# Two sequences' tokens at once: seven half products for the candidate's and the input gate's x part instead of eight

## The chip, the cores and the metric

The kernel runs on one core of a Trainium2 chip as one launch. The metric is device time in microseconds of one execution. The kernel before takes 2463.74 us, the median of three runs (2462.84 to 2463.92).

The engines are named as the profile names them: PE is TensorE's matmuls, PEld its weight loads, DVE VectorE, ACT ScalarE, POOL GpSimd, SP SyncE (which here mostly issues DMAs). Each engine works through its own instructions in order.

## The reference

The program is two layers on 32 sequences of 128 tokens of 512 values: layer 0 is a mixture of experts and a feed-forward part, layer 1 an expert stage that gives `r * y`, and then a recurrence. The change lies in the recurrence alone:

```python
x = x + L0_ffn(L0_cond(x, cond, ...), ...)
x = x + L1_ffn(L1_cond(x, token_ids, cond, ...), ...)

def L1_ffn(x, wf, uf, bf, wi, ui, bi, wc, uc, bc, wo, uo, bo, in_c):
    def step(c, xt):                       # x: (32, 128, 512); scan over the 32
        ft = sigmoid(xt @ wf.T + c @ uf.T + bf)
        it = sigmoid(xt @ wi.T + c @ ui.T + bi)
        gt = tanh(xt @ wc.T + c @ uc.T + bc)
        return ft * c + it * gt, None      # c: (128, 512)
    c_final, _ = lax.scan(step, broadcast(in_c), x)
    return tanh(x @ wo.T + c_final @ uo.T + bo)
```

One step takes one sequence: its 128 tokens are the batch, and the state c (128 x 512) goes from sequence to sequence. The x part of a gate, `xt @ w.T`, needs no c and can be computed ahead; the c part can't.

## The kernel before

All layers are one program. The change touches its last part, from the block `with sf:` (L1515) to the end of the body; the order of instructions ahead of it stays, but for one DVE instruction.

**Products in three parts.** A factor is split in a high part (ACT copies it to a shorter type, L64) and a low part (DVE subtracts that from the source, L65); `split` does both. `mm3` (L76 to L86, the matmul at L82) then multiplies high by high, high by low and low by high: three matmuls per block of 128 of the summed dimension. A product of 128 tokens x 512 by 512 x 512 is four blocks, so twelve matmuls with 128x512 results; a half product, over two blocks, is six.

**A step t of the recurrence** (loop at L1663). Three gates c, i, f, one PSUM bank each. `from_c` (L1591) adds the c part, `gate` (L1596) adds the bias on DVE (L1598), applies tanh or sigmoid on ACT (L1599) and multiplies i by c (L1601); `new_c` (L1602) makes the new c in two DVE instructions (L1604, L1606). PE must then wait for the new c, and gets other work in the meantime: the x part of c and i of step t + 1 (`from_x`, L1583, 24 matmuls), then the transposes of the new c (`turn`, ptC, L1578, followed by its split to cT), then the x part of f (12 matmuls) and the transposes of a later sequence (`gate_y`, ptF, L1566). So a step is 36 matmuls of the c part, 36 of the x part and eight transposes. The order is written out in the loop.

**Where z comes from.** z is `r * y` transposed and split. `get_y` (L1538 to L1546) gathers the rows of y on POOL's queue and loads r on SP's queue; `gate_y` (L1556) applies the sigmoid to r, multiplies (L1561), transposes, copies to zt (L1571), stores that to DRAM for the output stage (L1572) and splits it. `gate_y` runs two steps ahead (LEAD = 2). The last two of the eight groups of four sequences stay on the chip.

**Weights.** `weight` (L1494 to L1508) loads a matrix in two halves of 512 KB into a pool of raw tiles (`zop`, four slots) and splits each: casts of 128x1024 on ACT, subtracts on DVE. Before the stage, wc, uf and wi are loaded while the expert stage still runs, wf on POOL's queue during the first products; the expert stage's last outputs are copied by ACT to ob (L1465) and stored to `res_d`, from which y is gathered. wo is loaded after step 4.

**Banks of PSUM.** `ps_g` four (gates and output units), `ps_c` one (ptC), `ps_y` one (ptF), `ps_z` two (not used).

**The last steps and the output.** From step 29 on there is no x part left to do: the x part of step 31 is done at t = 29 and put by (L1688), and PE fills its waits for c with output units (`unit`, L1611: twelve matmuls with wo) of group 6, whose results ACT copies to SBUF. Then `cu` (L1724), the c part of the output from the last c and uo, then the other 28 units, group by group; groups 0 to 5 are loaded back (`fetch_z`, L1624) and split. `result` adds cu on DVE (L1729), applies tanh on ACT (L1732), adds x1 (L1733, by turns on DVE and POOL) and stores (L1734).

## Time and profile before

| | |
|---|---|
| median of three runs | 2463.74 us |
| the profiled execution's own time | 2462.88 us |
| its span in the profile | 2461.1 us |
| mean granted clock of TensorE | 0.995 |
| PE busy | 2421.7 us, 12870 matmuls |
| DVE busy | 1349.3 us, 2309 instructions |
| ACT busy | 1051.4 us, 1852 instructions |
| POOL busy | 408.9 us, 462 instructions |

The span runs from the first to the last instruction in the profile; 1.8 us of the execution lie around it. The recurrence takes the time from about 1795 to 2364 us of the span, the output from there to the end. Where the chain of waits is shown, a row is a start in us from the span's beginning, a length in us, an engine, the tile written, the line, and how many instructions. In the timeline, the square bracket behind a row tells how long the engine had been idle and which instruction released it. A clock of 1.00 is TensorE at its full clock.

### The profile page before, as it was taken

How to read it: one execution, taken by the hardware profiler on the slowest of the kernel's cores; microseconds unless marked ns; L12 is line 12 of the kernel's file. 1: busy time of each engine (PE TensorE's matmuls, PEld its weight loads, DVE VectorE, ACT ScalarE, POOL GpSimd, SP SyncE). 2: the span in 40 equal slices, each digit the busy share in tenths (PEclk: the TensorE clock that was granted, in tenths of full speed). 3: DMA queues.
4: the chain of work that ended last, by engine and by line, in shares of the span. 5: the costliest groups of instructions: out<-in, count | busy, mean ns of one | idle time of the engine just before them, and what ended most of it. 6: DMA issues, size and time to landing. Idle time of an engine off the chain costs nothing.

```text
span 2461.1 us, 36619 instructions
## 1 busy us (share of the span) xinstructions
PE 2421.7 (98%) x12870; PEld 2048.8 (83%) x12870; DVE 1349.3 (55%) x2309; ACT 1051.4 (43%) x1852; POOL 408.9 (17%) x462
## 2 busy tenths in 40 slices
PE   8999999999999999999999999999999999999998
PEld 6788788888888788888888889999978888888887
DVE  8896654556557454455454567667643333333363
ACT  5544533344224544455455466666532222222142
POOL 1000022221232233322223010000010000000012
PEclk9999999999999999999999999999999999999999
DMA  6445555557565343342342487777532111110164
GB/s 214 152 125 177 183 167 169 178 176 233 176 215 170 95 131 111 125 152 68 117 142 95 152 285 223 230 231 224 172 132 69 42 49 48 43 43 30 32 212 158
DMA packets 194125, 353.73 MB, mean 144 GB/s; under 512 B 37457, under 2 KB 70273, under 8 KB 191377
## 3 DMA queue, kind: packets, MB, share of 16 engines
q1 hardware_dynamic: 145392, 253.33, 31.4%
q0 software_dynamic: 36448, 75.95, 10.4%
q10 hardware_dynamic: 12096, 22.03, 2.5%
q8 instruction: 108, 1.77, 0.3%
q14 instruction: 81, 0.66, 0.1%
HBM read 374.99 MB, written 89.70 MB: 189 GB/s over the span
## 4 chain that ended last, share of the span: by engine, by line
PE 49%; issue 2%; DMA 1%; POOL 1%; DVE 1%; ACT 1%; POOLq 0%; DVEq 0%; ACTq 0%
PE phD L82 7%; PE ps_c L82 7%; PE ps_f L82 7%; PE ps_i L82 7%; PE poD L82 7%; PE po L82 3%; PE pb L82 2%; PE pv L82 2%; POOL hF L1733 1%; PE ptC L1578 1%; PE ptD L1431 1%; PE ptF L1566 1%; PE poF L82 0%; PE ptB L1256 0%; DMA rowsD<-xk_d,slot_t 0%
## 5 line engine op out<-in xcount | busy, mean ns | idle before, releaser
L65 DVE TENSOR_TENSOR wD<-rawD,wD 128x1024 fp32r<-128x1024 f32 x128 | 156.6, 1230 | 82.5 <-ACT wD L64 82.5
L82 PE MATMUL p<-xhl,swu 128*128 128x512 f32 x768 | 189.0, 397 | 5.9 <-ACT xhl L64 5.8
L82 PEld LDWEIGHTS phD<-xe,wD 128*128 128x128 f32 x1536 | 184.4, 189 | 2.1 <-ACT xe L64 0.9
L82 PE MATMUL phD<-xe,wD 128*128 128x256 f32 x1536 | 185.1, 281 | 0.7 <-ACT xe L64 0.7
L82 PE MATMUL p<-xhl,kept_u 128*128 128x512 f32 x768 | 184.3, 394 | 0.7 <-DVE kept_u L65 0.7
L82 PE MATMUL poD<-wD,hD 128*128 128x512 f32 x768 | 181.5, 392 | 0.0
L82 PEld LDWEIGHTS p<-xhl,swu 128*128 128x128 f32 x768 | 144.7, 190 | 36.1 <-ACT xhl L64 5.8
L82 PEld LDWEIGHTS p<-xhl,kept_u 128*128 128x128 f32 x768 | 141.9, 188 | 30.0 <-DVE kept_u L65 1.1
L82 PEld LDWEIGHTS poD<-wD,hD 128*128 128x128 f32 x768 | 141.9, 188 | 28.3
L64 ACT CAST wD<-rawD 128x1024 fp32r<-128x1024 f32 x128 | 133.3, 1046 | 56.0 <-PE poD L82 54.0
L290 POOL DMA_INDIRECT xg<-in_x_rows_dram,blk_t x71 | 67.6, 952 | 443.2 <-PE ptx L300 246.3
L1538 POOL DMA_INDIRECT y<-res_d,gat_i x32 | 30.4, 951 | 511.8 <-DVE r L1561 432.3
L82 PE MATMUL pur<-r,xb 128*128 x792 | 110.5, 288 | 4.2 <-ACT xb L64 1.1
L82 PE MATMUL por<-r,hbr 128*128 x396 | 107.9, 407 | 1.1 <-ACT hbr L64 1.1
L65 DVE TENSOR_TENSOR xb<-ptx,xb 128x512 fp32r<-128x512 f32 x68 | 47.0, 691 | 106.0 <-ACT xb L64 104.3
L82 PEld LDWEIGHTS pur<-r,xb 128*128 128x128 f32 x792 | 98.5, 189 | 6.4 <-issue 2.1
L82 PE MATMUL ps_f<-wf_hl,z 128*128 128x512 f32 x384 | 96.2, 399 | 0.0
L82 PE MATMUL ps_c<-uc_hl,cT 128*128 128x512 f32 x384 | 96.2, 399 | 0.0
L82 PE MATMUL ps_c<-wc_hl,z 128*128 128x512 f32 x384 | 94.8, 396 | 1.4 <-ACT z L64 1.4
L82 PE MATMUL pb<-rT,Wo_hl 128*128 128x256 f32 x768 | 95.2, 281 | 0.3 <-DVE rT L65 0.2
L82 PE MATMUL acc<-swd,as 128*128 128x512 f32 x384 | 94.7, 391 | 0.7 <-DVE as L65 0.6
L815 POOL DMA_INDIRECT o<-o_d,s_i x64 | 66.7, 1042 | 172.3 <-PE pth L835 84.4
(1020 smaller groups left out, 4991.3 us busy)
## 6 DMA issues: line engine op xcount, KB each, us to landing
rawD<-in_w_key_dram SPq DMA_DIRECT2D x64, 512.0 KB, 4.3
rawD<-in_w_value_dram SPq DMA_DIRECT2D x64, 512.0 KB, 4.3
swr<-in_sw_dram SPq DMA_DIRECT2D x120, 256.0 KB, 3.5
o_d<-obr SPq DMA_DIRECT2D x66, 256.0 KB, 2.4
rraw<-in_rw_dram SPq DMA_DIRECT2D x32, 256.0 KB, 3.1
xc<-in_x_dram SPq DMA_DIRECT2D x32, 256.0 KB, 3.6
hid_d<-o ACTq DMA_DIRECT2D x32, 256.0 KB, 2.2
xh_d<-xc SPq DMA_DIRECT2D x32, 256.0 KB, 2.8
```

What stands on the lines that cost most here:

```text
L64: first = nc.scalar.copy(hi, src).ins
L65: done = nc.vector.tensor_tensor(lo, src, hi.bitcast(F32), ALU.subtract).ins
L82: done = nc.tensor.matmul(ps, lhsT=left(hl, k), rhs=right(hr, k), start=start and k + n == 0, stop=stop and 3 * k + n == last,)
L290: nc.gpsimd.indirect_dma_start(out=xg[i], out_offset=None, in_=a["x_rows"], in_offset=bass.IndirectOffsetOnAxis(ap=blk_t[:, i : i + 1], ax ...
L815: nc.gpsimd.indirect_dma_start(out=o[n], out_offset=None, in_=o_d, in_offset=bass.IndirectOffsetOnAxis(ap=idx[:, b : b + 1], axis=0),)
L1431: nc.tensor.transpose(pt[:, k, :], xe[:, s, bass.ts(k, P)], ident)
L1538: got = nc.gpsimd.indirect_dma_start(out=y, out_offset=None, in_=res_d, in_offset=bass.IndirectOffsetOnAxis(ap=gat_i[:, b : b + 1], axis=0),)
L1566: nc.tensor.transpose(pt[:, k, :], r[:, bass.ts(k, P)], ident)
L1578: nc.tensor.transpose(pt[:, k, :], c[:, bass.ts(k, P)], ident)
L1733: (nc.gpsimd if n % 2 else nc.vector).tensor_tensor(h, h, x1s[g][:, :, o, :], ALU.add)
```

## The change

For two sequences 2n and 2n + 1, let A1, A2 be the halves of the first sequence's z along the summed dimension, B1, B2 the second's. Let c0, c1 and i0, i1 be the halves of wc and wi. Needed are four products of two halves each:

- first, c: A1 c0 + A2 c1; first, i: A1 i0 + A2 i1;
- second, c: B1 c0 + B2 c1; second, i: B1 i0 + B2 i1.

That is eight half products of six matmuls. After the change they are seven, as in the product of two 2x2 matrices with seven multiplications (Winograd's form): A1·c0, A2·c1, S1·T1, S2·T2, S3·T3, S4·i1, A2'·T4, where the S are sums of halves of z, made by DVE per pair, and the T are sums of halves of wc and wi, made once. (In the code the rows of the left matrix are the two sequences: A11, A12 the first's halves, "A22" the second half of the second's; B11 = c0, B21 = c1, B22 = i1.) The products are put together by eight more DVE additions per pair. The gate f keeps its plain product.

- **Pair 0** is computed plainly, c from B11 and B21 (12 matmuls), and i from B11, T1 = i0 - c0 and B22 (18 matmuls), since i0 itself is no longer kept. Pairs 1 to 15 take the seven products.
- **In the loop**, after an odd step five of the seven products (`first_of_pair`, 30 matmuls) stand ahead of the transposes of c and f's 12 behind; after an even step S3·T3 and f (6 + 12) stand ahead and A22·T4 (6) behind.
- **Two additions** of `second_i` are held behind the new c by an explicit order (`issue_after(made[0])`).
- **Weights**: nine half tiles in place of three whole pairs. B11, B21, T1, B22 and f0, f1 are made at the start; for T2, T3, T4 the halves of wi and wc are loaded again after step 0 (`rest_of_weights`). At t = 1 the bias of i becomes bi - bc.
- **z**: `gate_y` copies all of z to zt and stores all groups to DRAM; two are done after step 0, then one per step, three ahead. The first zt takes the buffer of the first cT.
- **Banks**: `ps_g` three, `ps_b` three (for the half products), `ps_c` and `ps_y` one each.
- **The end**: x parts go on to step 31, so no unit is left as filler there; wo is loaded at t = 28, uo after the loop; all eight groups are loaded back and computed in order, their units by turns in `ps_g` and `ps_b`; two units stand ahead of cu; the last result's addition of x1 is on DVE instead of POOL.

The diff, cut to its core:

```diff
+        def sums_z(n):
+            zt = zts[n]
+            a1, a2 = zt[:, 0, :K2], zt[:, 0, K2:]
+            b1, b2 = zt[:, 1, :K2], zt[:, 1, K2:]
+            s = gp.tile([P, 2, K2, P], F32, tag="sz", name=f"sz_{n}")
+            nc.vector.tensor_tensor(s[:, 0], b1, b2, ALU.add)
+            nc.vector.tensor_tensor(s[:, 1], s[:, 0], a1, ALU.subtract)
+            split(zS[n][:, 0:2, 0], zS[n][:, 0:2, 1], s)
+            nc.vector.tensor_tensor(s[:, 1], a2, s[:, 1], ALU.subtract)
+            nc.vector.tensor_tensor(s[:, 0], a1, b1, ALU.subtract)
+            split(zS[n][:, 2:4, 0], zS[n][:, 2:4, 1], s)
...
+        def first_of_pair(n):
+            first, second, c1 = (zop.tile([P, 2, D], F32, tag="raw", name=f"{x}_{n}") for x in ("ta", "tb", "pa"))
+            p1, u, v = first[:, 0], first[:, 1], second[:, 0]
+            nc.vector.tensor_tensor(p1, block("A11", "B11", n), bias["c"], ALU.add)
+            nc.vector.tensor_tensor(c1[:, 0], block("A12", "B21", n), p1, ALU.add)
+            nc.vector.tensor_tensor(v, block("S1", "T1", n), bias["i"], ALU.add)
+            nc.vector.tensor_tensor(u, block("S2", "T2", n), p1, ALU.add)
+            nc.vector.tensor_tensor(v, v, u, ALU.add)
+            nc.vector.tensor_tensor(c1[:, 1], block("S4", "B22", n), v, ALU.add)
+            parts[2 * n] = {"c": c1[:, 0], "i": c1[:, 1]}
+            half_done[n] = u, v
+
+        def second_i(n):
+            c2 = zop.tile([P, 2, D], F32, tag="raw", name=f"pd_{n}")
+            u, v = half_done[n]
+            p7 = block("S3", "T3", n)
+            with tc.issue_after(made[0]):
+                nc.vector.tensor_tensor(u, p7, u, ALU.add)
+                nc.vector.tensor_tensor(c2[:, 1], p7, v, ALU.add)
+            parts[2 * n + 1] = {"c": c2[:, 0], "i": c2[:, 1]}
+
+        def second_c(n):
+            u, _ = half_done.pop(n)
+            nc.vector.tensor_tensor(parts[2 * n + 1]["c"], block("A22", "T4", n), u, ALU.add)
...
+        c0, i0 = raw_part("wc", 0), raw_part("wi", 0)
+        split_part("B11", c0)
+        c1 = raw_part("wc", 1)
+        split_part("B21", c1)
+        nc.vector.tensor_tensor(i0, i0, c0, ALU.subtract)
+        split_part("T1", i0)
+        i1 = raw_part("wi", 1)
+        split_part("B22", i1)
         uc["f"] = weight("uf", uf_p, zop, 4)
-        wx["i"] = weight("wi", wx_p, zop, 4, pair=wx_hl["i"])
...
+        def rest_of_weights():
+            with tc.issue_after(last_r[0]):
+                i0, i1, c0, c1 = (raw_part(n, h) for n in ("wi", "wc") for h in range(2))
+            nc.vector.tensor_tensor(i0, i1, i0, ALU.subtract)
+            nc.vector.tensor_tensor(c0, i0, c0, ALU.add)
+            split_part("T2", c0)
+            nc.vector.tensor_tensor(c1, c1, c0, ALU.subtract)
+            split_part("T3", i0)
+            split_part("T4", c1)
...
-            if t < NB - 2:
-                from_x(t + 1, ps, "ci", True, False)
-            cT_next = turn(c, t + 1)
-            if t < NB - 2:
-                from_x(t + 1, ps, "f", True, False)
-            for b in ((t + LEAD,) if t < NB - 4 else (NB - 2, NB - 1) if t == NB - 4 else ()):
+            n, odd = divmod(t + 1, 2)
+            if t == 0:
+                for w in "ci":
+                    plain(1, ps, w, True, False)
+                cT_next = turn(c, t + 1)
+                plain(1, ps, "f", True, False)
+            elif t < NB - 1:
+                if odd:
+                    second_i(n)
+                    plain(t + 1, ps, "f", True, False)
+                else:
+                    first_of_pair(n)
+                cT_next = turn(c, t + 1)
+                if odd:
+                    second_c(n)
+                else:
+                    plain(t + 1, ps, "f", True, False)
+            else:
+                cT_next = turn(c, t + 1)
+            for b in (2, 3) if t == 0 else (t + 3,) if t + 3 < NB else ():
                 gate_y(b)
                 if b + LEAD < NB:
                     get_y(b + LEAD)
+                if b % 2:
+                    sums_z(b // 2)
+            if t == 0:
+                rest_of_weights()
```

`block` is six matmuls of one half product into a bank of `ps_b`, `plain` the six-matmul halves added into a gate's bank, `raw_part` one load of 512 KB into a slot of `zop`, and `split_part` its split.

## The prediction

> **What bounds the kernel now.** I read the page's busy shares first. TensorE (PE) works 98% of the span, so time moves by what PE no longer does or by holes that open in it.

> ```profile
> PE 2421.7 (98%) x12870; PEld 2048.8 (83%) x12870; DVE 1349.3 (55%) x2309; ACT 1051.4 (43%) x1852; POOL 408.9 (17%) x462
> ```

> Then busy time by stretch of the last stage (columns: stretch, us, busy us and instructions of PE, PEld, DVE, ACT, POOL; granted clock; DMA share; GB/s). The recurrence is one stretch without a hole; its start and the turn to the output products run at a lower mean clock:

> ```profile
> 1828.00:2346.00 518.00, 518.00 (x2396) 428.27 (x2395) 187.61 (x273) 125.83 (x204) 24.56 (x26) 1.00 0.16 50
> 1795.00:1813.00 18.00, 14.93 (x59) 11.63 (x58) 6.87 (x8) 9.13 (x14) 7.28 (x10) 0.84 0.66 225
> 2367.00:2388.00 21.00, 20.44 (x101) 18.01 (x100) 14.68 (x23) 11.04 (x23) 3.84 (x3) 0.84 0.77 257
> ```

> Third, the chain of waits inside the recurrence (start, us, what). It never leaves PE: twelve matmuls take 2.72 us, so one takes 2.72 / 12 = 0.2267, and four transposes 0.44.

> ```profile
> 2318.77 2.72 PE ps_f L82 x12
> 2321.49 2.72 PE ps_c L82 x12
> 2324.21 2.72 PE ps_i L82 x12
> ...
> 2335.09 0.44 PE ptC L1578 x4
> ```

> A step of 72 matmuls and two sets of transposes takes 72 x 0.2267 + 0.88 + about 0.05 = 17.25 us, while DVE is busy 187.6 / 518 x 17.25 = 6.2 us and ACT 4.2.

> Last, the timeline of one step, for what stands between the last product and the next transposes:

> ```profile
> 1836.84 0.69 DVE L1598 TENSOR_TENSOR v_f<-ps_f,bf_bc 128x512 f32<-128x512 f32 x1 [0.64 <-PE ps_f L82]
> 1837.56 0.63 ACT L1599 ACTIVATE v_f<-v_f 128x512 f32<-128x512 f32 x1 [2.09 <-DVE v_f L1598]
> 1838.23 0.69 DVE L1604 TENSOR_TENSOR v_f<-v_f,c 128x512 f32<-128x512 f32 x1 [0.70 <-ACT v_f L1599]
> 1838.95 0.69 DVE L1606 TENSOR_TENSOR c<-v_f,v_i 128x512 f32<-128x512 f32 x1
> 1842.08 0.60 PE L1578 MATMUL ptC<-ident,c 128*128 128x128 f32 x4
> ```

> Call T the end of f's matmuls (1836.64, where the next PE row starts). The state c is ready at T + 3.00; ptC comes at T + 5.44: 24 matmuls cover the gate with 2.4 us to spare.

> **1. Matmuls: -17.7 us.** Eight half products (48 matmuls) per pair become seven (42) for 15 pairs: 90 fewer. Pair 0 stays plain with three halves for i instead of two, 6 more in each of two sequences: +12. 78 x 0.2267 = 17.7, at full clock and with PE never waiting. Groups of six instead of twelve should not cost more each: the expert stage changes its output tile every six matmuls and runs 36 in 8.42 us with the overlapped end of its last (8.42 - 0.23 = 8.19, or 0.2275 each).

> ```profile
> 1695.33 8.42 PE L82 MATMUL poD<-wD,hD 128*128 128x512 f32 x36
> ```

> **2. The steady steps: 0.** Added per pair on DVE: 8 adds of 128x512 (the row of L1598, 0.69; the gates keep their own adds, with another operand): 5.5 us; two splits of 128x512 (DVE 0.69 each, ACT 0.59) and four 128x256 adds at 0.42 (the layer-0 rows of that size). That is 5.5 + 1.4 + 1.7 = 8.6 us a pair, 4.3 a step: DVE goes to some 10.5 of a 16.6 us step, ACT to 5. Neither fills. What counts is order:
> - First kind of step (odd t; filler 30 matmuls, then ptC at T + 6.80). DVE does v_f's add, then A11's add (T + 1.56 to 2.25) ahead of v_f times c: c at T + 4.39, 2.4 us to spare. A11's bank is wanted back at T + 4.08 and A12's at T + 5.44; their adds end at 2.25 and about 3.7.
> - Second kind (even t; filler 6 + 12, ptC at T + 4.08). The two adds on p7 are held behind new c, so c stays at T + 3.00: 1.1 us to spare. The split of c's transpose ends at T + 6.0 (0.59 and 0.69 after ptC); from_c starts at T + 6.3 and uses its low half at T + 6.8.
> The cover is thus 1.1 us in every other step; if it is gone, each microsecond beyond it costs 15.

> **3. Start of the stage: +4.4 (+2 to +7).** In the order of the built program ACT copies the expert outputs ob ahead of the weight casts (it was the other way round), and uf's two raw halves need slots of a pool of four that the c and i halves hold.

> ```profile
> 1795.69 0.58 ACT L1465 COPY ob<-poD 128x512 f32<-128x512 f32 x1
> ...
> 1803.76 0.69 DVE L1561 TENSOR_TENSOR r<-y,r 128x512 f32<-128x512 f32 x1 [6.72 <-DMA y<-res_d,gat_i]
> ...
> 1808.38 1.22 PE L82 MATMUL ps_c<-wc_hl,z 128*128 128x512 f32 x2 [1.37 <-ACT z L64]
> ...
> 1810.25 4.22 PE L82 MATMUL ps_c<-wc_hl,z 128*128 128x512 f32 x10
> ```

> Before, all casts of uf, wc and wi were done when ob was copied. Now five casts of 1.05 us (B11, B21, T1, B22 and uf's first half) follow it; one of them stands ahead of the second store of ob, which moves the gather of y by 1.05. uf's loads leave at about 1799.7 and 1801.3 and land 4.7 to 7.0 later (rows of wc and uf); behind them on ACT stand the two casts of wf, whose loads on POOL's queue are now behind two bias loads and land at about 1809; their casts end at 1810.95. Then come r_2's sigmoid 0.63, zt 0.59, z's cast 0.62: the first x products start near 1812.95 instead of 1808.38, and the ten of c at 1814.7 instead of 1810.25: +4.4. Low end: loads as quick as wc's and wf's fastest. High end: the uf loads as slow as 7.0 with the casts behind them, which adds 2.5.

> **4. The rest of the weights: +4.3 (0 to +7).** T2, T3, T4 are made from wi and wc read again, issued on SP's queue behind r_5's load, which waits for ptF_3 (about 1838.5). Four loads of 512 KB that landed in 3.3 to 4.7 us at the same rate before are there at 1843 to 1847. DVE takes its queue in order: a subtract and an add of 128x1024 and three low halves at 1.22 stand ahead of v_f times c of step 1 or 2. I make c ready at 1854.4 where PE could transpose at 1851.9: 2.5, and 0.3 for a bank of the same chain; both nearest to the cast rows. A gap also lowered the clock at the start (half clock for the 4.22 us of ten matmuls that take 2.27): I add 1.5 for a part of such a stretch. Low end: the loads 3 us earlier, no gap. High end: 4 us and a whole stretch (2.0 to 3.4).

> **5. The turn to the output, and the end: +1.3 - 0.6 (-4 to +5).** Before, from the end of the last f (2360.64) to 2452.5 the matmuls' own time falls 4.2 us short, by one gap and the low clock after it:

> ```profile
> 2366.78 2.79 PE L82 MATMUL cu<-cT,uo_hl 128*128 128x128 f32 x24
> 2370.14 5.16 PE L82 MATMUL cu<-cT,uo_hl 128*128 128x128 f32 x24 [0.56 <-ACT cu L1724]
> ```

> Now uo's casts and the casts of zF_1 and zF_2 stand in ACT's and DVE's queues ahead of step 31's sigmoid and products. I make c ready at T + 5.6 with ptC reached at T + 4.3 (1.35 wait), 0.45 for c's low half, 0.85 at cu_3 and the same low clock after it (2.8): 5.5 instead of 4.2. If the clock stays up there, it is 4 less. The last sum moves from POOL (1.26 us at L1733) to DVE (0.69): -0.6.

> **Weighed against the trace.** The clock fell to 0.50 at 2372 to 2376 although PE's gap before was 0.56 us. [...]

> **Sum.** -17.7 + 4.4 + 4.3 + 1.3 - 0.6 = -8.3. The profiled execution took 2462.88 us (span 2461.1, 1.8 around it), so 2454.6; the median of the three runs is 2463.74, 0.9 above, so 2455.4. I say 2455.0.

> **Rivals.**
> - The edges are hidden: terms 3 to 5 at their low ends, +2, 0 and -4 to 0, leave -17.7 + 2 - 2.5 to 0: 2445 to 2448. For it: loads here land anywhere from 3.3 to 7.0 us. Against: ACT's order at the start is fixed.
> - The edges take most of it: high ends +7, +7, +4 make -17.7 + 18 = 0; half-way to them, 2459 to 2464, within 0.2%. For it: three places where in-order queues meet fresh loads.
> - Slower: the steady steps stall. Place: ptC of the second kind of step, or the third bank of S2 and S4. Price: 15 us for each microsecond of DVE delay beyond the 1.1 spare; from 0.9 beyond it (2.0 in all) the sum passes +4.9. If short gaps of each pair cost a half-clock stretch as at 2370 (5.16 us for 24 matmuls against 2.79, so 2.4 to 3.4), it is 15 x 3 - 8 = +37: 2500. Against: the adds on p7 are held back behind new c, and the gaps are none if the order above holds. [...]
> - The products save nothing, because six matmuls and a change of tile cost what eight do: 2475. The poD row excludes nearly all of it.

> **Chances.** Forecast (2449 to 2459) 0.53; edges hidden 0.18; edges take most 0.19; steady stall 0.08; nothing saved 0.02. A measurement of this kernel can tell about 0.2%, 4.9 us: faster below 2458.8, slower above 2468.7. So faster 0.71, same 0.19, slower 0.10. The range takes in the hidden and the dear edges: 2446 to 2464; the stall lies outside.

> **What would show it.** 78 fewer PE instructions, all steps between 1830 and 2350 without PE idle at clock 1.00 and 16.6 us mean; DVE at about 10.5 us a step; ps_c's ten matmuls of t = 0 4 us later; one wait of ptC for c near 1852; one at step 31. Wrong if ptC waits for DVE in every even step, if the granted clock between 1860 and 2340 is below 1.00, or if p and S tiles show idle before them released by DVE.

## The result and the profile after

The changed kernel takes 2453.65 us (median of 6 runs, 2447.08 to 2457.65) against 2464.26 for the kernel before (6 runs, 2462.84 to 2468.64): the medians are 10.6 us apart, and the ratio of the runs is 0.995, with a 95% interval of 0.9934 to 0.9966. The forecast was 2455.0, faster.

The profiled execution of the changed kernel took 2457.65 us, its slowest run, so its span (2456.0) is only 5.1 us shorter. The order of instructions ahead of the last stage is the same in both kernels, and yet the stage's first product (`ps_c<-uc_hl`) starts at 1801.10 instead of 1795.70: 5.4 us. I don't count them to the change. The low-clock stretches ahead of it (where the granted clock is 0.5) add up to 13.7 us instead of 6.8, worth 3.4 us by an estimate (half of the 6.8 more, at a granted clock of 0.5), and in the other profiles of the changed kernel and its versions the stage starts anywhere from 1794.2 to 1804.0 us. With only two profiles of the kernel before (1795.7 and 1795.9) this is likely and not shown. So all that follows is measured from that first product to the end of the span: 654.9 us after, 665.4 before, 10.5 less.

First the page's line of busy shares: 78 matmuls fewer, and 239 DVE instructions more, 140 us.

```profile
PE 2407.7 (98%) x12792; PEld 2036.4 (83%) x12792; DVE 1488.9 (61%) x2548; ACT 1079.0 (44%) x1897; POOL 412.0 (17%) x461
```

Then busy time by stretch (columns as before): the steady steps, the start, and steps 1 and 2, where T2, T3 and T4 are made.

```profile
1890.00:2340.00 450.00, 450.00 (x2086) 372.24 (x2085) 280.80 (x444) 131.43 (x215) 24.54 (x22) 1.00 0.15 47
1801.10:1832.00 30.90, 23.07 (x87) 17.35 (x86) 15.49 (x17) 15.82 (x20) 10.71 (x11) 0.89 0.63 213
1832.00:1883.40 51.40, 47.10 (x209) 38.51 (x209) 34.34 (x53) 18.43 (x29) 4.04 (x4) 0.93 0.31 103
```

In the steady steps PE has no hole and the clock is 1.00, with DVE busy 62% of the time. Both edges have holes. The waits of PE between 1790 us and the end name them (us in total, times, longest):

```profile
PE ptF L1572 <- ACT zt L1574: 6.8, 2, 3.5
PE ps_f L82 <- ACT uf_hl L64: 2.8, 2, 2.4
PE ps_f L82 <- DVE uf_hl L65: 1.8, 2, 1.0
PE ptC L1594 <- DVE c L1675: 1.4, 2, 0.8
PE cu L82 <- ACT cu L1849: 0.5, 1, 0.5
```

The timeline shows where they stand. At the start ACT casts the halves of wc behind the copies of ob; uf's first load leaves at 1804.12, f's c part waits for it, wf's casts follow, and zt_0's copy comes behind all of them:

```profile
1801.78 1.05 ACT L64 CAST wB_hl<-raw_wc 128x1024 fp32r<-128x1024 f32 x1
...
1804.12 0.33 SPq L1504 DMA_DIRECT2D raw_uf<-in_uf_dram  x1
...
1809.13 0.49 PE L82 MATMUL ps_f<-uf_hl,cT 128*128 128x512 f32 x1 [2.43 <-ACT uf_hl L64]
...
1820.19 0.66 PE L1572 MATMUL ptF<-ident,r 128*128 128x128 f32 x4 [3.26 <-ACT zt L1574]
```

In step 1 the weights read again land late, and zt_4's copy stands behind three casts of them on ACT; PE stands at the transposes that need its bank:

```profile
1855.21 1.23 DVE L1722 TENSOR_TENSOR raw_wi<-raw_wi,raw_wi 128x1024 f32<-128x1024 f32 x1 [3.12 <-DMA raw_wi<-in_wi_dram]
...
1861.43 0.58 ACT L1574 COPY zt<-ptF 128x512 f32<-128x512 f32 x1
...
1862.06 1.11 PE L1572 MATMUL ptF<-ident,r 128*128 128x128 f32 x4 [3.50 <-ACT zt L1574]
...
1863.97 1.11 PE L1594 MATMUL ptC<-ident,c 128*128 128x128 f32 x4 [0.80 <-DVE c L1675]
```

At the end there are two short waits and, unlike before, no low clock behind them (the stretch 2355 to 2370 has 1.00).

For the comparison of runs the stage is cut by its transposes of c. ptC_n is the start of the transposes of c_n; every run has the same four pieces (us, from the PE rows of each profile):

| run | first product to ptC_1 | ptC_1 to ptC_5 | ptC_5 to ptC_30 | ptC_30 to the end | stage |
|---|---|---|---|---|---|
| before | 29.1 | 69.2 | 441.0 | 126.2 | 665.4 |
| changed | 37.8 | 75.5 | 415.8 | 125.8 | 654.9 |
| e1 plain pairs | 37.5 | 69.7 | 432.3 | 130.4 | 669.9 |
| e2 weights early | 38.5 | 68.2 | 415.8 | 125.9 | 648.5 |
| e3 T3, T4 later | 39.4 | 72.9 | 415.8 | 125.9 | 653.9 |
| e4 uf first | 32.8 | 73.6 | 415.8 | 125.9 | 648.1 |
| e5 both | 32.5 | 68.2 | 415.8 | 126.3 | 642.9 |
| e6 changed again | 38.8 | 73.6 | 415.8 | 126.0 | 654.1 |
| e7 one more on DVE | 38.7 | 73.8 | 415.8 | 130.4 | 658.7 |
| e8 three more on DVE | 38.6 | 74.9 | 420.0 | 126.2 | 659.7 |
| e9 before again | 29.3 | 69.2 | 442.5 | 126.8 | 667.9 |
| e10 last add on POOL | 38.5 | 73.1 | 415.8 | 128.8 | 656.2 |
| e11 both, cu mixed | 32.5 | 68.3 | 415.8 | 125.4 | 642.0 |
| e12 six more on DVE | 38.5 | 77.9 | 420.5 | 131.4 | 668.1 |

The kernel before does step 31's x part (36 matmuls, 8.2 us) in the third piece, the changed kernel (24 matmuls, 5.4 us) in the fourth. All output units lie in the fourth piece in both.

### The profile page after: what moved, and what is told of

It reads as the page before. It is cut to its first block, busy times and chain, and to the rows that moved or that the text cites. A ratio compares the mean times of both kernels' runs of the same rounds, so it can differ in the third digit from the quotient of the medians.

```text
span 2456.0 us, 36828 instructions
## 1 busy us (share of the span) xinstructions
PE 2407.7 (98%) x12792; PEld 2036.4 (83%) x12792; DVE 1488.9 (61%) x2548; ACT 1079.0 (44%) x1897; POOL 412.0 (17%) x461
## 3 DMA queue, kind: packets, MB, share of 16 engines
q0 software_dynamic: 36448, 75.95, 10.4%
## 4 chain that ended last, share of the span: by engine, by line
PE 53%; DMA 2%; DVE 1%; ACT 1%; issue 0%; SPq 0%; POOL 0%; DVEq 0%; ACTq 0%
PE phD L82 7%; PE poD L82 7%; PE ps_f L82 7%; PE po L82 4%; PE ps_c L82 4%; PE ps_i L82 4%; PE poF L82 3%; PE pS L82 3%; PE pb L82 2%; PE pA L82 2%; PE pv L82 2%; PE ptC L1594 1%; PE ptD L1431 1%; PE ptF L1572 1%; PE ptB L1256 0%; PE pr L1176 0%
## 5 line engine op out<-in xcount | busy, mean ns | idle before, releaser
L82 PE MATMUL p<-xhl,swu 128*128 128x512 f32 x768 | 189.1, 397 | 5.7 <-ACT xhl L64 5.7
L82 PEld LDWEIGHTS phD<-xe,wD 128*128 128x128 f32 x1536 | 185.5, 190 | 2.1 <-ACT xe L64 0.9
L82 PE MATMUL phD<-xe,wD 128*128 128x256 f32 x1536 | 186.2, 282 | 0.7 <-ACT xe L64 0.7
L82 PE MATMUL p<-xhl,kept_u 128*128 128x512 f32 x768 | 184.2, 394 | 0.7 <-DVE kept_u L65 0.7
L82 PE MATMUL poD<-wD,hD 128*128 128x512 f32 x768 | 181.6, 392 | 0.0
L82 PEld LDWEIGHTS p<-xhl,swu 128*128 128x128 f32 x768 | 144.7, 190 | 36.1 <-ACT xhl L64 5.7
L82 PEld LDWEIGHTS p<-xhl,kept_u 128*128 128x128 f32 x768 | 141.9, 188 | 30.0 <-DVE kept_u L65 1.1
L82 PEld LDWEIGHTS poD<-wD,hD 128*128 128x128 f32 x768 | 141.9, 188 | 28.3
L64 ACT CAST wD<-rawD 128x1024 fp32r<-128x1024 f32 x128 | 133.4, 1047 | 56.8 <-PE poD L82 35.0
L1540 POOL DMA_INDIRECT y<-res_d,gat_i x32 | 36.5, 1140 | 489.4 <-DVE r L1564 410.9
L82 PE MATMUL pur<-r,xb 128*128 x792 | 111.8, 290 | 4.4 <-issue 1.5
L82 PE MATMUL por<-r,hbr 128*128 x396 | 108.2, 408 | 1.3 <-ACT hbr L64 1.2
L82 PEld LDWEIGHTS pur<-r,xb 128*128 128x128 f32 x792 | 99.6, 190 | 6.9 <-issue 2.9
L82 PE MATMUL ps_f<-uf_hl,cT 128*128 128x512 f32 x384 | 94.2, 393 | 4.6 <-ACT uf_hl L64 2.8
L82 PE MATMUL ps_c<-uc_hl,cT 128*128 128x512 f32 x384 | 96.2, 398 | 0.0
L82 PE MATMUL pb<-rT,Wo_hl 128*128 128x256 f32 x768 | 95.2, 281 | 0.3 <-DVE rT L65 0.2
L82 PE MATMUL acc<-kept_d,as 128*128 128x512 f32 x384 | 93.5, 391 | 1.2 <-ACT as L64 0.7
L82 PE MATMUL pv<-w_recept_hl,xr 128*128 128x512 f32 x384 | 94.4, 395 | 0.0
```

The costliest lines, as they stand in the source:

```text
L64: first = nc.scalar.copy(hi, src).ins
L82: done = nc.tensor.matmul(ps, lhsT=left(hl, k), rhs=right(hr, k), start=start and k + n == 0, stop=stop and 3 * k + n == last,)
L1540: got = nc.gpsimd.indirect_dma_start(out=y, out_offset=None, in_=res_d, in_offset=bass.IndirectOffsetOnAxis(ap=gat_i[:, b : b + 1], axis=0),)
```

## The experiments

**e1: all pairs plain.** What do the seven products bring by themselves?

```diff
-                "i": ((0, "B11"), (0, "T1"), (1, "B22")),
+                "i": ((0, "T1"), (1, "B22")),
-        nc.vector.tensor_tensor(i0, i0, c0, ALU.subtract)
...
-            if t == 0:
+            if t < NB - 1:
                 for w in "ci":
-                    plain(1, ps, w, True, False)
+                    plain(t + 1, ps, w, True, False)
...
-                if b % 2:
-                    sums_z(b // 2)
-            if t == 0:
-                rest_of_weights()
```

> All pairs as plain products: c and i take 24 matmuls of x part per sequence again, no sums of z, no T2, T3, T4, the bias of i unchanged; banks, loads at the start, filler places and the end as in the changed kernel. Theory A (each matmul left out is worth 0.2267 us, steady steps have no stall, the weights read again cost about 7.2 us): 2453.65 + 17.7 - 7.2 = 2464.2, within 3 us of the kernel before; steady step 17.25 us; no PE wait near 1860. Theory B (the seven products save nothing, the gain came from the new end of the kernel): 2446 to 2454.

Measured: 2466.2 us against 2463.5 before, ratio 1.0011 (1.0000 to 1.0021). Theory A holds; two transposes of c in a row stand 17.29 us apart:

```profile
2005.14 0.60 PE L1594 MATMUL ptC<-ident,c 128*128 128x128 f32 x4
...
2022.43 0.60 PE L1594 MATMUL ptC<-ident,c 128*128 128x128 f32 x4
```

In the third piece the seven products save 432.3 - 415.8 = 16.5 us, where the 72 matmuls that it holds fewer (1728 instead of 1800) make 16.3 at 0.2267. The new start is still there without them (37.5), the wait in step 1 is not (69.7): the one comes with the half tiles and their loading, the other with T2 to T4. The start even holds 12 matmuls (2.7 us) fewer than in the changed kernel; in this profile the low clock there lasts 13.7 us, in the changed kernel's 6.8.

**e2: the weights read again, early.**

```diff
+        with tc.issue_after(last_r[0]):
+            raws = [raw_part(n, h) for n in ("wi", "wc") for h in range(2)]
         cT_next = cT
         for t in range(NB):
...
-            with tc.issue_after(last_r[0]):
-                i0, i1, c0, c1 = (raw_part(n, h) for n in ("wi", "wc") for h in range(2))
-            nc.vector.tensor_tensor(i0, i1, i0, ALU.subtract)
+            i0, i1, c0, c1 = raws
+            with tc.issue_after(made[0]):
+                nc.vector.tensor_tensor(i0, i1, i0, ALU.subtract)
```

> The four loads for T2, T3, T4 are issued ahead of the loop instead of after r_5's load, and their sums on DVE start behind c_1. Theory A (PE waits at 1858 to 1865 because the loads land at 1855 and their casts then stand ahead of zt_4 and of v_f times c): the waits of 3.5 and 0.8 us go and so does the low clock behind them, 6 to 7 us faster than the changed kernel, 2446.5 to 2448. Rival (the order of the queues alone makes the wait, loads or not): the wait moves to step 0 or 1, 2452 to 2455.

Measured: 2443.46 us, ratio 0.992 (0.9904 to 0.9935). The second piece is 68.2, 7.2 less than in the changed kernel's first profile and 5.4 less than in its second, and the low clock near 1862 is gone. For the wait, theory A holds. The median fell by 10.2, to 3.0 below the expected range, which is more than the stage shows (5.6 to 6.4 us shorter). Between the two profiled executions, 4.7 of 11.1 us lie ahead of the stage: it starts at 1796.4 us of the span in this profile and at 1801.1 and 1799.1 in the two of the changed kernel.

**e3: the same late loads, T3 and T4 behind c_2.**

```diff
             split_part("T2", c0)
-            nc.vector.tensor_tensor(c1, c1, c0, ALU.subtract)
-            split_part("T3", i0)
-            split_part("T4", c1)
+            return i0, c0, c1
...
+                with tc.issue_after(made[0]):
+                    nc.vector.tensor_tensor(c1, c1, c0, ALU.subtract)
+                    split_part("T3", i0)
+                    split_part("T4", c1)
```

> Loads as in the changed kernel; only T4's subtraction and the splits of T3 and T4 are put behind c_2, since they are used a step later than T2. If the queue of casts is what holds zt_4 and c: wait of 1 to 2 us left, 2 to 6 us faster than the changed kernel, 2448 to 2451.5. If the late loads alone decide (T2 itself comes too late): no change, 2452 to 2455.

Measured: 2449.72 us, ratio 0.9941 (0.9925 to 0.9956). The time lies in the range of the first theory, but the profile doesn't bear it out: the waits at ptF and ptC in step 1 are gone, and one of 3.0 us stands earlier, where S2·T2 needs the bank that A11's addition frees, and that addition now stands on DVE behind work that waits for the late loads:

```profile
1859.79 0.76 PE L82 MATMUL pS<-wT_hl,z 128*128 128x512 f32 x1 [3.04 <-DVE ta L1637]
```

The second piece is 72.9, only 0.7 to 2.6 less than in the changed kernel. So the late loads decide, and the order behind them chooses where PE stands. The 3.9 us by which the median is lower are explained by this stretch in part at most.

**e4: uf first.**

```diff
+        uc["f"] = weight("uf", uf_p, zop, 4)
         c0, i0 = raw_part("wc", 0), raw_part("wi", 0)
...
         split_part("B22", i1)
-        uc["f"] = weight("uf", uf_p, zop, 4)
```

> uf is loaded and cast ahead of the halves of wc and wi instead of behind them. Theory A (f's c part waits for uf at the start, then the gather and wf's casts queue behind): the start's loss against the kernel before falls from 6.0 us to 1 to 3, total 2448.5 to 2451. Rival (wf, loaded on POOL's queue behind the bias rows, sets the start whatever uf does): the first ten x products of c start as late as before, 2453 to 2455.

Measured: 2444.08 us, ratio 0.9921 (0.9905 to 0.9937). The first piece falls by 5.0, to 32.8; less the 12 matmuls of pair 0's plain i (2.7) that is 1.0 above before. PE no longer waits for uf at all; what is left is one wait for zt_0's copy behind the first of wf's casts (4.7 us), where the kernel before also had its waits (1.7 us at ptF, 1.4 at the first x product). For the start, theory A holds. The median is 4.4 below the expected range; between the profiled executions, the stage is 6.0 to 6.8 us shorter and the rest lies ahead of it.

**e5: e2 and e4 together.**

> uf first and the four loads ahead of the loop, together. By the profiles of the two alone, measured from the first c part of the stage to its end (654.9 us in the changed kernel), the one takes 5.0 us off the start and the other 7.2 off steps 1 and 2: theory A (two separate queues of casts, so the gains add): 642.7 us of stage, 11 to 13 us faster than the changed kernel on the same chip. Rival (both cure the same wait, or the early loads now collide with wf and z): 6 to 9 us faster.

Measured: 2441.62 us, ratio 0.9906 (0.9891 to 0.9922); the changed kernel measured beside it 2454.10 (e6, below): 12.5 us less, and a stage of 642.9 us where 642.7 was expected. The gains add, so the two waits were two. All waits of PE that are left in the stage:

```profile
PE ptF L1572 <- ACT zt L1574: 4.6, 1, 4.6
PE ptC L1594 <- DVE c L1675: 1.0, 1, 1.0
PE cu L82 <- ACT cu L1851: 0.5, 1, 0.5
```

**e6: the changed kernel once more**, for a second profile of it.

> The changed kernel once more, as it is, on the same chip as the others of this call: 2453.65 give or take 2; stage of 654.9 us, no low clock after 2300 us of the span, waits of 3.5 and 0.8 us near the stage's 61st to 63rd us.

Measured: 2454.10 us (2453.66 to 2456.27), ratio 0.9955 (0.9941 to 0.9969). The stage takes 654.1; the waits at ptF are 2.1 at the longest, at ptC 1.3, not 3.5 and 0.8. So the loss in step 1 is 5.4 to 7.2 us, by the execution.

**e7 and e8: one and three more DVE instructions** between c and its transposes in steps 4, 6, ... 30:

```diff
             made[:] = [nc.vector.tensor_tensor(new, v["f"], v["i"], ALU.add).ins]
+            for _ in range(N if t >= 4 and t % 2 == 0 and t < NB - 1 else 0):
+                made[:] = [nc.vector.tensor_tensor(new, new, new, ALU.max).ins]
```

> One more DVE instruction of 128x512 (c = max(c, c), about 0.69 us) between c and its transposes in steps 4, 6, ... 30. Theory A (1.08 us to spare there): no change, within 1 us of the changed kernel. Rival (DVE is already the bound of those steps): +0.69 x 14 = 9.7 us.

Measured: third piece 415.8, as without it: 1.08 us of cover held 0.69. The median was 2457.31, ratio 0.9959 (0.9945 to 0.9973), 3.2 above e6 where at most 1 was expected, but with an interval that overlaps e6's; in its profile the last piece is 4.4 us longer, 3.4 of it, by an estimate, from the low clock told of below (0.50 from 2371.7 to 2378.5 us, and half of these 6.8), the rest from longer waits at ptC_32 (1.2 us) and among cu's products (1.0).

> Three such instructions (2.07 us). Theory A: 2.07 - 1.08 = 0.99 us of wait at ptC in each of 14 steps, 13.9 us at full clock. If each such gap also lowers the granted clock for a stretch of 3.4 us (1.7 lost) or two (3.4 lost): 38 or 62 us in all. [...]

Measured: 2459.82 us, ratio 0.9978 (0.9967 to 0.9990): 5.7 more than e6, not 13.9. The wait at ptC is there in 13 steps, but of 0.18 us:

```profile
2010.96 1.07 PE L82 MATMUL pA<-wT_hl,z 128*128 128x512 f32 x4
2012.21 0.63 PE L1594 MATMUL ptC<-ident,c 128*128 128x128 f32 x4 [0.18 <-DVE c L1677]
2012.59 0.72 PE L82 MATMUL pA<-wT_hl,z 128*128 128x512 f32 x2
```

The order of the built program has changed with the added work: four of the six matmuls of A22·T4 now stand ahead of ptC. That is 0.9 us more cover. The bracket doesn't show the whole loss: the third piece is 4.2 us longer with four matmuls (0.9) fewer in it, some 0.4 us for each of the 12 such waits in it. The price of delay in these steps is thus not one for one.

**e9: the kernel before once more.**

> The kernel before once more, for its profile. If the low clock behind the first gap among cu's products belongs to the old order of the end (100.7 us from the last matmul of the recurrence to the end), it is there again. If it hangs on chance in each execution, it may be missing, and then that stretch is 3.4 us shorter, 97.3, and the changed kernel's end has gained only some 2 us, not 5.5.

Measured: 2465.41 us, one run. The low clock at the end is there again (6.8 us from 2374.0), with a gap of 0.48 us among cu's products before it and one of 0.67 across its start; from the last matmul of f to the end it takes 101.4 us, 100.7 in the first profile. Two of two fit the old order as the cause, but e1 and e7 have the low clock with the new end too, so chance is not excluded. The third piece is longer than in the first profile by one wait of 1.4 us at ptC.

**e10: the last addition on POOL.**

```diff
-            add = nc.gpsimd if n % 2 and not last else nc.vector
+            add = nc.gpsimd if n % 2 else nc.vector
```

> The last result's addition of x1 on POOL again, all else as in the changed kernel. From the last matmul's end to the end of the span it takes 5.82 us in the changed kernel, 8.60 before. If the instruction's own time is the difference (1.26 against 0.69): 6.4. If POOL at the very end costs more than its instruction: 8.6.

Measured: 2454.64 us, one run; from the last matmul to the end 8.60 us, as before, against 5.82. 2.8 us hang on which engine works last; its instruction is only 0.6 of it. First e10's last instruction, then the changed kernel's:

```profile
2445.87 1.26 POOL L1860 TENSOR_TENSOR hF<-hF,x1F 128x512 f32<-128x512 f32 x1 [4.14 <-ACT hF L1858]
...
2451.62 0.69 DVE L1860 TENSOR_TENSOR hF<-hF,x1F 128x512 f32<-128x512 f32 x1 [0.69 <-ACT hF L1858]
```

POOL's closing instruction (DRAIN) ends 5.0 us behind its last addition, 0.8 before the end of e10's span, and from 3.0 us before the end on it is the only engine that has not yet closed. In the changed kernel it also ends 5.0 us behind POOL's last addition, but that is an earlier one, so nothing waits for it. What POOL waits for, the trace doesn't show.

**e11: e5 with two output units between cu's products.**

```diff
             nc.scalar.activation(cu[:, o, :], pc, AF.Identity, bias=bo1[:, o : o + 1])
+            if o % 2 == 0:
+                unit(0, 2 + o // 2)
```

> The version with uf first and early loads, and the third and fourth unit of group 0 put between the four products of cu instead of behind them. If the low clock at the end comes from a stretch of PE with little work (six us of matmuls with 128 columns and a gap of 0.5 us), it can't occur now: stage 642 us or a little less, 0 to 1.5 us faster than that version's 2441.6 in the median. Rival: cu's results come later and hold the first results: 1 us slower.

Measured: 2439.29 us (2436.26 to 2446.88), ratio 0.9894 (0.9877 to 0.9910). The stage is 0.9 shorter than e5's, the wait at cu is gone; the medians can't be told apart. It has the lowest median here: 1.06% below the kernel before, where the change as it was made gives 0.5%. As e5's profile has no low clock at the end either, this pair doesn't show what the mixing does to the clock.

**e12: six more DVE instructions** in the same steps, to open gaps.

> Six more DVE instructions between c and its transposes in 14 steps: 4.14 us later, so PE idles some 1.3 us at ptC and some 0.9 us before from_c in each of them, 2.1 us a step at full clock, 29 us in all. [...] If the clock is decided on a fixed grid of 3.41 us, by how busy PE was in the last cell (below about a half), with a phase that drifts against the steps: low cells behind 4 to 10 of the 14 gaps and behind none of the undisturbed steps, 1.7 us each on top: 36 to 46 us in all.

Measured: 2468.73 us, one run. The third piece is 4.7 us longer with 12 matmuls (2.7) fewer in it, so some 7 us where 29 were expected over the steps: the built order put A22·T4, a ptF and six of the next pair's 30 first products ahead of ptC, and the waits in the steady steps are short. So the theory of the grid is not tried there. At ptC_31, with no next pair left to fill, PE waits 2.4 us, and the clock is low behind that one gap (two stretches of 3.4 us, columns as before):

```profile
2351.50:2354.90 3.40, 1.14 (x6) 0.60 (x4) 3.30 (x6) 2.17 (x4) 0.00 (x0) 1.00 0.52 175
2354.90:2358.40 3.50, 3.07 (x9) 2.30 (x10) 2.75 (x5) 2.19 (x6) 0.00 (x0) 0.51 0.91 309
```

PE was idle for 2.3 us within the first, and the second runs at 0.51.

## Why the prediction was right, step by step

- **Matmuls, -17.7: right.** 78 fewer on the page; between e1 and the changed kernel, 72 matmuls of the third piece are worth 16.5 us, 16.3 by the forecast's price. Groups of six cost what groups of twelve do.
- **Steady steps, 0: right.** No idle time of PE between 1890 and 2340; DVE is busy 280.8 / 450 x 16.63 = 10.4 us a step (10.5 forecast), ACT 4.9 (5). There are nine additions per pair and not the eight that I had counted (L1637 to L1642, L1652, L1653 and L1658, 15 of each); the busy time comes out lower all the same, as additions back to back start 0.60 us apart while each row lasts 0.68. The order in the step was right to 0.2 us: c is ready at T + 4.2 and T + 3.0, ptC starts at T + 6.80 and T + 4.08. The cover of 1.1 us is confirmed by e7. The price named for the time beyond it, 15 us for each microsecond, failed: 1 us beyond (e8) cost 5.7 us, because the order of the built program moves filler to where the wait would be. The rival of stalling steps was dearer on paper than e8 shows it.
- **Start, +4.4: right mechanism, too small.** 37.8 - 29.1 - 2.7 (12 matmuls of pair 0) = 6.0, within the bounds of 2 to 7. uf behind the other weights was the cause of most of it (e4: -5.0).
- **Rest of the weights, +4.3: too small, and by another wait.** 5.4 to 7.2 (e2). I had the transposes of c wait for DVE's queue; the long wait is at ptF, for zt_4's copy behind three casts on ACT's queue. The loads, which I put at 3.3 to 4.7 us by the start's rows, took about 9 (issued from 1846.26 on, both halves of wi there at 1855.2). Issued 23 us earlier, in e2, wc's halves took 8.2 as well. e3 shows that with loads so late the one other order tried helps little; e2, that loads in time cure it.
- **The end, +1.3 - 0.6: wrong sign.** The last piece took 0.3 us less with 24 matmuls (5.4) more in it: -5.8. Of that 2.8 is the last addition on DVE (e10), which I had priced by its instruction alone, and 3.4 (an estimate, half of the 6.8 us at 0.50 in the profile before) is the low clock, which I had kept ("the same low clock after it") and which cu's products escape in nine of the eleven profiles with the new end (all but e1 and e7; e11 not counted), while both profiles of the kernel before have it. I had named the case that the clock stays up (4 less) and left it out of the sum. The waits were shorter than forecast too: 0.6 us at ptC_32 for 1.35, 0.5 at cu for 0.85.
- **The sum.** -17.7 + 6.0 + 7.2 - 5.8 = -10.3 against 10.5 measured in the stage, and -8.3 forecast. The two edges were 4.5 too cheap and the end 6.5 too dear: the total is right partly by luck, because these errors cancel. Among the rivals, the hidden edges were summed with -2.5 for term 5 where its low end is named as -4; with -4 they reach down to 2444.

The 1.5 us for a low clock in term 4 was right in kind. The wait of 3.5 us in step 1 was followed by 6.8 us of low clock in the first profile, waits of 2.1 and 1.3 by 3.4 us in the second; at half clock that is 3.4 and 1.7 us lost, by an estimate.

## What to carry to other kernels

When a kernel is bound by one engine, count its instructions first and then spend the effort on the edges: here the algebra gave 17.7 us, and its count held (16.5 for 16.3 where it was measured), while two places near the stage's start, where casts queue up behind loads, took 13 back, and two edits of a few lines brought 12.5 of them home. A load placed by "when it is first needed" should be placed by when its buffers come free: the four loads could go 23 us earlier (22 us behind the stage's first product instead of 45) at no cost that e2 shows. And cover measured in one order of instructions is not fixed: where a planner orders them, a longer wait can bring its own filler, as in e8 (5.7 us for the 13.9 expected).

## What the runs showed of the hardware

| PE busy in the cell | cells | next at half clock |
|---|---|---|
| under 0.4 | 36 | 36 |
| 0.4 to 0.5 | 21 | 15 |
| 0.5 to 0.6 | 34 | 7 |
| 0.6 to 0.9 | 259 | 5 |
| 0.9 and more | 9484 | 7 (all near 100 us of the span) |

So 2.28 us without PE at 923.85 in the profile before, all in one cell (1.13 us busy of 3.41), had half clock behind them, as had e12's 2.3 us; 1.85 us without PE at 1117.2 in the changed kernel's profile lay across two cells, with 2.99 and 1.99 us busy, and the clock stayed at 1.00. In the changed kernel's step 1:

```profile
1858.30:1861.70 3.40, 0.26 (x3) 0.02 (x1) 3.40 (x4) 2.17 (x3) 0.00 (x0) 1.00 0.22 80
1861.70:1865.10 3.40, 2.24 (x9) 1.84 (x10) 3.40 (x6) 2.13 (x4) 0.00 (x0) 0.51 0.34 128
1865.10:1868.60 3.50, 3.50 (x9) 2.72 (x9) 2.13 (x5) 1.74 (x3) 0.00 (x0) 0.50 0.35 100
```

**Half clock came behind small matmuls without a gap.** These are the seven cells of 0.9 and more. Near 100 us all these kernels run the same 32 matmuls with 16x16 results (`ps_z`), 2.15 us by the rows, with no gap around them. In the seven executions where at least 2.09 us of them fall into one cell, the next cell is at half clock; in the seven where the grid parts them so that at most 1.82 us lie in one, it is not. First e6, where the cell begins with them, then the changed kernel, where it begins 0.33 us after them:

```profile
100.52 2.15 PE L419 MATMUL ps_z<-ident,zt 16*128 16x16 f32 x32
100.50:103.90 3.40, 3.40 (x39) 3.13 (x39) 1.16 (x3) 0.93 (x3) 0.00 (x0) 1.00 0.91 296
103.90:107.30 3.40, 3.40 (x10) 2.62 (x9) 2.74 (x7) 1.49 (x4) 0.00 (x0) 0.51 0.53 144
...
100.14 2.15 PE L419 MATMUL ps_z<-ident,zt 16*128 16x16 f32 x32
103.90:107.30 3.40, 3.40 (x16) 2.81 (x16) 3.23 (x8) 1.42 (x3) 0.00 (x0) 1.00 0.64 183
```

Whether the few columns, the few rows or the kind of matmul makes the difference, the runs don't show. For matmuls with 128 columns there is an estimate only. Among the five cells of 0.6 to 0.9, four lie in cu's products at the end: 18 to 23 matmuls, all but one of them with 128 columns, and 0.6 to 1.0 us without PE. Counted by columns, at 0.2267 us for 512, these matmuls fill 0.30 to 0.43 of the cell (an estimate); the other cells made up mostly of cu's products, which no half clock follows, come to 0.38 and more. Half clock comes there with the new end too, in e1 and e7, where the longest gap among cu's products is 0.69 and 1.04 us instead of the changed kernel's 0.52; in e7:

```profile
2368.30:2371.70 3.40, 2.36 (x22) 2.22 (x21) 2.70 (x5) 2.79 (x6) 0.00 (x0) 1.00 0.66 252
2371.70:2375.10 3.40, 3.40 (x15) 3.19 (x15) 3.14 (x5) 3.07 (x8) 1.59 (x1) 0.50 0.29 28
```

That the few columns are why is argued from the cells, not tried alone. A low cell costs some 1.7 us while PE works through it, by an estimate: half of 3.41, and at the start of the kernel before ten matmuls, mostly within such a stretch, took 4.22 us instead of the 2.27 at 0.2267 each. Behind the 16x16 matmuls it came or not by where the cells lay. That such cells are why executions of one program differ by 10 us is not shown: of the changed kernel's two profiles the slower one has less low clock between its first and last matmul (27.3 us against 34.1), and the two of the kernel before have the same (20.5).
